# A Winograd convolution pair on one core: two positions of the second convolution also filtered along columns, the map between them kept for two chunks

## The chip, the cores and the metric

The kernel runs on one core of a Trainium2 chip. A core has a matrix engine (TensorE, PE in the profile; PEld is its loading of weights), VectorE (DVE), ScalarE (ACT), GpSimd (POOL), SyncE (SP), which here only issues transfers, and 16 DMA engines. Each engine works through its own list of instructions in the order of the program. All data is fp32; matmuls write to PSUM, everything else stays in SBUF, 128 partitions wide. The metric is the device time of one launch in microseconds, the median of several runs.

## The reference

Four layers on x of shape (4, 256, 56, 56). Layers 0 and 2 are involutions, layer 3 filters in the frequency domain, and each layer normalises its input by group first and adds its result to it. Layer 1 is what the change touches:

```python
h = group_norm(x)
y = conv3x3(h, w1)                      # 256 -> 256 channels, padding 1
y = relu(bn(y, g1, b1, rm1, rv1))
y = conv3x3(y, w2)                      # 256 -> 256
y = bn(y, g2, b2, rm2, rv2)
x = x + relu(h + y)
```

The running statistics of bn are constants, so bn is a scale and a shift for each channel.

## The kernel before

**Where.** `conv_layer` holds layer 1 (L1183 to L1806), from 507 to 1201 us of the span; layer 2 follows. Each image is cut into three row chunks for each convolution, twelve for the four images: `C1_ROWS` 20, 18 and 18 rows, `C2_ROWS` 16, 20 and 20. The order of chunks is conv1(0), then conv1(i) and conv2(i-1) for i from 1 to 11, then conv2(11). So an image's period holds three first and three second chunks.

**Winograd along the rows' width.** A row of 56 is 14 tiles of 4 outputs. `transform` (L1382 to L1425, VectorE) makes six planes of each input row; the 3x3 filters are transformed to six positions in the same way (`row_weights`, `summed_weights`). The product of position k is a sum over 2 blocks of 128 input channels and 3 filter rows, made for 2 blocks of output channels (co); a chunk of n rows has n x 14 columns for each co. The order of positions is `KS` = 1, 2, 3, 4, 0, 5. The output transform puts the six products together to four outputs of each tile. For rows that two chunks share, the transformed planes are copied from the chunk before (`known` rows, L1386 on ScalarE).

**Filtering along columns too.** In the first convolution a position can be "filtered": two output rows come of four products in place of six. It needs sums of input rows: inner ones (row 1 plus row 2, row 2 minus row 1; VectorE, L1464 and L1465) and outer ones (row 0 minus row 2 and row 1 minus row 3; a ScalarE product by -1, L1457, and an accumulating DMA that POOL issues, L1458; for chunk 1 VectorE at L1455). It also needs sums of the filters' rows (`column_weights` on VectorE, L1316 to L1318, and `filter_weights` on ScalarE, L1309). conv1(0) filters none, conv1(1) five positions, all later chunks six. The 16 matmuls of a filtered position are at L1520. Their products come together by a ScalarE copy of the first inner one from PSUM (L1529) and three VectorE operations (L1533, L1534, L1536).

**The second convolution** filters none: 12 matmuls (L1482) for each position, over both co in one PSUM tile for positions 1 to 4, then positions 0 and 5 for co 0, then both for co 1. VectorE combines at L1643 to L1666. Then `joined(co)` sends each half on: ScalarE scales and shifts the four outputs (L1603), POOL adds x by an accumulating DMA (L1604); in the next chunks ScalarE applies the relu (L1606), POOL adds x once more (L1607) and SP stores (L1608). For the last two chunks x is loaded to SBUF beforehand, and `residual` (L1587, ScalarE) makes group norm plus shift in one buffer, from which VectorE goes on (L1611, L1616). The sums for layer 2's norm are `bn_stats` on VectorE (L1633).

**Buffers.** `ph1` holds the normalised input of one chunk (22 rows), written by ScalarE's `phases` (L1379). `ph2` holds the whole image's map between the convolutions (58 rows), written by the first convolution's `outputs` (L1500). Inner sums share four slots, outer sums four. PSUM gives the convolutions four tiles of two banks; a filtered position takes two of these, an unfiltered pair one.

**What sets the order.** There is no scheduler: each chunk has twelve lists of work, `after[0]` to `after[11]`, run after each half position, and work of neighbouring chunks is put into them by `place` and `append` (the loop over `order`). `in_order` then holds each engine to that order of the program. `late_r` carries the relu, addition and store of an output half to the following chunks' lists. SP also issues the loads of input rows (`load_rows`, L1164).

Of the kernel before, what the change touches and what calls it, by code (L numbers as in the profile page):

```python
# [16 lines left out]
P = 128  # L17
B, C, H, W = 4, 256, 56, 56
NB = C // P
# [36 lines left out]
C1_ROWS = [(0, 20), (20, 38), (38, 56)]  # L56
# [16 lines left out]
def net_kernel(  # L73
# [1109 lines left out]
    def conv_layer(xin, xout, st, ahead):  # L1183
        with ExitStack() as es:
# [51 lines left out]
            v2_sb = wpool.tile([P, 2 * NY], F32, name="v2_sb")  # L1236

            def new_v2(half):

                n_v2[half] += 1  # L1240
                at = (n_v2[half] - 1) % 4
                if half:
                    return [room["v2"][:, at * NY : (at + 1) * NY]]
                if at == 3:
                    return [room[r][:, 5 * NY : 5 * NY + NY // 2] for r in ("v2", "xr")]
                t = room["v2"][:, 4 * NY : 5 * NY] if at == 2 else v2_sb[:, at * NY : (at + 1) * NY]
                return [t[:, : NY // 2], t[:, NY // 2 :]]
# [63 lines left out]
            def column_weights(ci, k0, k1):  # L1311

                w0, w1, w2 = (u1_sb[:, ci, y, k0:k1, :] for y in range(3))
                x = between_weights(ci, k0, k1)
                s = y_tile(5 if k0 == 5 else 3)[:, : (k1 - k0) * C].rearrange("p (k n) -> p k n", n=C)
                tt(s, w0, w2, ALU.add)  # L1316
                tt(x, s, w1, ALU.subtract)
                tt(w1, s, w1, ALU.add)  # L1318


            PL, VP = (0, 2, 1, 3), (0, 1, 2, 3, 5, 4)
            ph1 = wpool.tile([P, 4, CV_ROWS + 2, NB, WT + 1], F32, name="ph1")
            ph2 = wpool.tile([P, 4, H + 2, NB, WT + 1], F32, name="ph2")
# [3 lines left out]
            for j in range(4):  # L1327
                for y in (0, H + 1):
                    nc.gpsimd.memset(ph2[:, j, y], 0.0)
# [33 lines left out]
            def phases(i):  # L1363

                y0, y1, lo, hi = rows1(i)
                n, r0, known = y1 - y0 + 2, lo - (y0 - 1), 2 if i % 3 else 0
# [5 lines left out]
                for ci in range(NB):  # L1372
                    at = ci * (CV_ROWS + 2) * W
                    xr = room["rows"][:, at + known * W : at + (hi - lo) * W].rearrange("p (r t j) -> p j r t", t=WT, j=4)
                    for j in range(4):
                        q, t0 = (j + 1) % 4, (j + 1) // 4
                        dst = ph1[:, PL[q], r0 + known : r0 + hi - lo, ci, t0 : t0 + WT]
                        s, t = rstd[:, ci : ci + 1], shift[:, ci : ci + 1]
                        nc.scalar.activation(dst, xr[:, j], AF.Identity, bias=t, scale=s)  # L1379
                        yield  # L1380

            def transform(v, ph, y0, n, known):  # L1382

                if known is not None:
                    old, m = known
                    nc.scalar.copy(  # L1386
                        v[:, :, : 2 * NB].rearrange("p k r t -> p k (r t)"),
                        old[:, :, m * NB : (m + 2) * NB].rearrange("p k r t -> p k (r t)"),
                    )
                    v, y0, n = v[:, :, 2 * NB :], y0 + 2, n - 2  # L1390
# [36 lines left out]
            v_sb = [wpool.tile([P, WPOS, (CV_ROWS + 2) * NB, WT], F32, name=f"v{k}") for k in range(2)]  # L1427

            def input1(i):
# [3 lines left out]
                known = (v_of[1, i - 1], p1 - p0) if i % 3 else None  # L1433
                yield from transform(v, ph1, 0, y1 - y0 + 2, known)

            def input2(i):
                y0, y1 = C2_ROWS[i % 3]
                v = v_of[2, i] = v_sb[i == n_chunks - 1]
                p0, p1 = C2_ROWS[i % 3 - 1]
                known = (v_of[2, i - 1], p1 - p0) if i % 3 else None  # L1440
                yield from transform(v, ph2, y0, y1 - y0 + 2, known)

            def columns(i, k, half):

                y0, y1, _, _ = rows1(i)
                n = y1 - y0
                m = n // 2
                v = v_of[1, i][:, VP[k]]
                if half:
                    (t,) = new_v2(1)  # L1450
                    v = v.rearrange("p r t -> p (r t)")
                    at = slice(0, n * NB * WT)
                    below = slice(2 * NB * WT, (n + 2) * NB * WT)
                    if i == 1:
                        tt(t[:, at], v[:, at], v[:, below], ALU.subtract)  # L1455
                    else:
                        nc.scalar.mul(t[:, at], v[:, below], -1.0)  # L1457
                        nc.gpsimd.dma_start(t[:, at], v[:, at], accum_op=ALU.add)  # L1458
                    t = t.rearrange("p (r e n) -> p e r n", e=2, n=NB * WT)
                    v2_of[i, k, 1] = [t[:, e] for e in range(2)]  # L1460
                else:
                    v = v.rearrange("p (r e c) t -> p e r (c t)", e=2, c=NB)
                    t = v2_of[i, k, 0] = [x.rearrange("p (r n) -> p r n", n=NB * WT) for x in new_v2(0)]
                    tt(t[0][:, :m], v[:, 1, :m], v[:, 0, 1 : m + 1], ALU.add)  # L1464
                    tt(t[1][:, :m], v[:, 0, 1 : m + 1], v[:, 1, :m], ALU.subtract)  # L1465


            FIRST = [(k, half) for k in KS[:4] for half in range(2)]
# [16 lines left out]

            def conv1(i, after, tail):
# [3 lines left out]
                m = n // 2 * WT  # L1490
                a, t, b, s, q = (y_tile(k)[:, : NB * n * WT] for k in (0, 1, 2, 5, 4))
                first = s if i else q
                home = {1: s, 2: q, 3: t, 4: s, 0: y_tile(3)[:, : NB * n * WT], 5: s}

                def outputs(*js):
                    for j in js:
                        o = (a, t, b, q)[j].rearrange("p (c r t) -> p c r t", c=NB, t=WT)
                        p, t0 = PL[(j + 1) % 4], (j + 1) // 4
                        for co in range(NB):
                            nc.scalar.activation(  # L1500
                                ph2[:, p, y0 + 1 : y1 + 1, co, t0 : t0 + WT],
# [7 lines left out]
                for n_s, k in enumerate(KS):  # L1509
                    if k in filtered(i):  # L1510
                        va = v2_of[i, k, 0]
                        vb = v2_of[i, k, 1]
                        ux = [between_weights(ci, k, k + 1)[:, 0] for ci in range(NB)]
                        u0, u1, u2 = ([u1_sb[:, ci, y, k] for ci in range(NB)] for y in range(3))
                        inner, outer = two_banks(), two_banks()
                        work4 = ((inner, 0, va, 0, u1), (inner, 1, va, 1, ux), (outer, 0, vb, 0, u0), (outer, 1, vb, 1, u2))
                        for ps, bank, v2, e, u in work4:
                            for co in range(NB):
                                for ci in range(NB):
                                    nc.tensor.matmul(  # L1520
                                        ps[:, bank, co * m : (co + 1) * m],
                                        u[ci][:, co * P : (co + 1) * P],
                                        v2[e][:, : n // 2, ci * WT : (ci + 1) * WT],
                                        start=(ci == 0),
                                        stop=(ci == NB - 1),
                                    )
                        o = home[k].rearrange("p (r e t) -> p e r t", e=2, t=WT)
                        m1, m2 = (inner[:, e, : NB * m].rearrange("p (r t) -> p r t", t=WT) for e in range(2))
                        nc.scalar.copy(o[:, 0], m1)  # L1529
                        for late in filtered(i)[n_s + 4 : n_s + 5]:  # L1530
                            columns(i, late, 0)
                            columns(i, late, 1)
                        tt(o[:, 1], o[:, 0], m2, ALU.subtract)  # L1533
                        tt(o[:, 0], o[:, 0], m2, ALU.add)  # L1534
                        run_all(after[2 * n_s])
                        tt(o, o, outer[:, :, : NB * m].rearrange("p e (r t) -> p e r t", t=WT), ALU.add)  # L1536
# [30 lines left out]
            def conv2(i, after, sums, tail):  # L1567
# [7 lines left out]
                p, t, r, q = (y_tile(k)[:, : NB * m] for k in range(4))  # L1575
                both = lambda x: x.rearrange("p (c r) -> p c r", c=NB)

                res = ux_sb.rearrange("p c k n -> p (c k n)")[:, : n * W]
                summed = i < n_chunks - 2

                def residual(co):
# [4 lines left out]
                    x = xr_of[i, co][:, : n * W]  # L1586
# [8 lines left out]
                def joined(co):  # L1595

                    y = room["h"][:, : 4 * NY].rearrange("p (j n) -> p j n", j=4)[:, :, co * m : (co + 1) * m]
                    if summed:
# [4 lines left out]
                        nc.scalar.activation(x.rearrange("p (q j) -> p j q", j=4), y, AF.Identity, bias=t, scale=s)  # L1603
                        nc.gpsimd.dma_start(x, xin[bb][co][:, at], accum_op=ALU.add)  # L1604
                        k, by = 5 + 2 * co, rstd[:, co : co + 1]
                        late_r[k].append(lambda: nc.scalar.activation(x, x, AF.Relu, scale=by))  # L1606
                        late_r[k + 1].append(lambda: nc.gpsimd.dma_start(x, xin[bb][co][:, at], accum_op=ALU.add))  # L1607
                        late_r[k + 4].append(lambda: nc.sync.dma_start(xout[bb][co][:, at], x))  # L1608
                        return
                    rj = res.rearrange("p (j q) -> p j q", j=4)  # L1610
# [24 lines left out]
                for n_s, k in enumerate(KS[:4]):  # L1635
                    pair = two_banks()
                    for co in range(NB):
                        unfiltered(pair[:, co, :m], u2_sb, v, k, co, n)
                        if co == 0:
                            run_all(after[2 * n_s])  # L1640
                    got = pair[:, :, :m]
                    if k == 1:
                        nc.scalar.copy(both(q), got)  # L1643
                    elif k == 2:
                        tt(both(p), both(q), got, ALU.add)
                        tt(both(q), got, both(q), ALU.subtract)
# [238 lines left out]
```

## Time and profile before

| | |
|---|---|
| median of 3 runs | 1740.52 us (1738.83 to 1744.15) |
| the profiled execution, its own time | 1735.74 us |
| its span in the profile | 1733.9 us |
| PE busy over the span | 1664.7 us, 96% |
| DVE busy | 1317.1 us, 76% |
| ACT busy | 933.5 us, 54% |
| POOL busy | 476.4 us, 27% |
| L1482, the unfiltered matmuls | 422.8 us |
| L1520, the filtered matmuls | 159.7 us |
| mean granted clock of TensorE | 0.984 |

The page describes one execution. Busy times are summed over the engine's instructions; L1482 is line 1482 of the kernel before. Each matmul of the program appears in the trace as two records, so 12 matmuls are 24 records. The chain that ended last is followed back from the last instruction, each time to what released it; its shares say which lines set the length. A wait is idle time of an engine just before an instruction, put down to what ended it. A window is a stretch of the span, counted from its start, with each engine's busy time in it.

### The profile page before, as it was taken

How to read it: one execution, taken by the hardware profiler on the slowest of the kernel's cores; microseconds unless marked ns; L12 is line 12 of the kernel's file. 1: busy time of each engine (PE TensorE's matmuls, PEld its weight loads, DVE VectorE, ACT ScalarE, POOL GpSimd, SP SyncE). 2: the span in 40 equal slices, each digit the busy share in tenths (PEclk: the TensorE clock that was granted, in tenths of full speed). 3: DMA queues.
4: the chain of work that ended last, by engine and by line, in shares of the span. 5: the costliest groups of instructions: out<-in, count | busy, mean ns of one | idle time of the engine just before them, and what ended most of it. 6: DMA issues, size and time to landing. Idle time of an engine off the chain costs nothing.

```text
span 1733.9 us, 56359 instructions
## 1 busy us (share of the span) xinstructions
PE 1664.7 (96%) x24296; PEld 1479.3 (85%) x24296; DVE 1317.1 (76%) x2467; ACT 933.5 (54%) x2024; POOL 476.4 (27%) x669
## 2 busy tenths in 40 slices
PE   6999999999999999999999999998999899999998
PEld 4998998888977999898899889986988788788886
DVE  2777787777769887798878888856787678778775
ACT  2655556456646455443455245325667567577564
POOL 2223322323334111211122111100000563563571
PEclk9999999999989999999999999999999999999996
DMA  2455444543659546454565354553444666664652
GB/s 89 129 167 162 137 151 160 166 129 103 220 184 260 95 106 142 76 125 96 119 143 97 82 118 92 100 167 104 147 142 151 206 208 196 210 209 161 203 161 103
DMA packets 89030, 252.15 MB, mean 145 GB/s; under 512 B 14453, under 2 KB 35966, under 8 KB 85070
## 3 DMA queue, kind: packets, MB, share of 16 engines
q1 hardware_dynamic: 57438, 163.33, 29.1%
q0 software_dynamic: 30304, 83.95, 22.6%
q8 instruction: 192, 3.15, 0.8%
q10 hardware_dynamic: 1040, 1.26, 0.3%
q14 instruction: 56, 0.46, 0.1%
HBM read 95.07 MB, written 49.15 MB: 83 GB/s over the span
## 4 chain that ended last, share of the span: by engine, by line
PE 70%; DVE 15%; DMA 4%; ACT 4%; issue 3%; SPq 2%; POOL 2%; ACTq 0%; POOLq 0%; DVEq 0%
PE mm L1482 22%; PE ps L593 14%; PE ps L635 14%; PE mm L1520 11%; DVE kt L611 5%; PE ps L407 3%; DVE un L655 3%; DMA xw<-xw 2%; DMA u_sb<-in_wc_dram 2%; PE ps L469 2%; DVE st L1105 1%; ACT hp L488 1%; SPq L425 1%; ACT kt L604 1%; PE ps L718 1%
## 5 line engine op out<-in xcount | busy, mean ns | idle before, releaser
L1482 PE MATMUL mm<-v,u_sb 128*128 128x280 f32 (+2 forms) x1896 | 422.8, 384 | 0.7 <-DVE xs L1534 0.7
L1482 PEld LDWEIGHTS mm<-v,u_sb 128*128 128x128 f32 x1896 | 357.8, 189 | 62.2 <-issue 1.7
L635 PE MATMUL ps<-kt,xw 126*32 126x48 f32 (+1 forms) x12544 | 378.9, 235 | 20.9 <-issue 8.2
L635 PEld LDWEIGHTS ps<-kt,xw 126*32 126x32 f32 (+1 forms) x12544 | 340.6, 121 | 65.8 <-issue 41.5
L593 PE MATMUL ps<-hp,z_sb 64*126 64x133 f32 x6144 | 385.2, 279 | 9.2 <-DVE kt L611 5.0
L593 PEld LDWEIGHTS ps<-hp,z_sb 64*126 64x126 f32 x6144 | 365.1, 186 | 25.7 <-DVE kt L611 7.1
L611 DVE TENSOR_TENSOR kt<-ps,zb_sb 126x798 f32<-126x798 f32 x352 | 333.0, 980 | 59.4 <-PE ps L593 59.0
L604 ACT ACTIVATE kt<-ps,zb_sb 126x133 f32<-126x133 f32 x960 | 281.0, 442 | 108.4 <-PE ps L593 108.4
L655 DVE SCALAR_TENSOR_TENSOR un<-ps,s,un 128x240 f32<-128x240 f32 x224 | 102.4, 457 | 83.4 <-ACT un L650 79.3
L1520 PE MATMUL mm<-xs,u_sb 128*128 128x126 f32 (+1 forms) x1296 | 159.7, 277 | 4.4 <-DVE xs L1534 2.6
L655 DVE SCALAR_TENSOR_TENSOR un<-ps,par_sb,un 128x240 f32<-128x240 f32 x224 | 97.5, 456 | 82.0 <-ACT un L648 78.1
L1520 PEld LDWEIGHTS mm<-xs,u_sb 128*128 128x128 f32 x1296 | 153.3, 191 | 5.4 <-issue 2.9
L660 POOL TENSOR_TENSOR xs<-un,xs 128x240 f32<-128x240 f32 x112 | 72.1, 665 | 216.1 <-DVE un L655 216.1
L419 ACT COPY xw<-ps 126x896 f32<-126x896 f32 x112 | 101.4, 906 | 41.7 <-DMA xw<-xw 22.8
L1458 POOL DMA_DIRECT2D xs<-v x60 | 52.8, 1015 | 249.4 <-ACT xs L1457 248.5
L407 PE MATMUL ps<-ident_sb,strip_sb 128*126 128x128 f32 x784 | 111.6, 282 | 7.7 <-issue 4.3
L150 POOL TENSOR_TENSOR norm_sb<-norm_sb,mhalf 128x1 f32<-128x1 f32 x32 | 19.2, 601 | 360.5 <-DVE norm_sb L149 360.5
L648 ACT ACTIVATE un<-ps,par_sb 128x240 f32<-128x240 f32 x112 | 50.3, 449 | 119.4 <-PE ps L635 109.8
L650 ACT ACTIVATE un<-ps,bn_t,s 128x240 f32<-128x240 f32 x112 | 60.2, 538 | 88.2 <-PE ps L635 80.0
L407 PEld LDWEIGHTS ps<-ident_sb,strip_sb 128*126 128x126 f32 x784 | 84.2, 140 | 19.5 <-issue 5.4
L1603 ACT ACTIVATE xs<-hp,raw,raw 128x1120 f32<-128x1120 f32 (+1 forms) x20 | 45.2, 2260 | 97.7 <-DVE hp L1666 97.7
L1379 ACT ACTIVATE ph<-xs,norm_sb 128x294 f32<-128x294 f32 (+2 forms) x96 | 80.7, 865 | 9.5 <-DMA xs<-x 7.6
(291 smaller groups left out, 2010.0 us busy)
## 6 DMA issues: line engine op xcount, KB each, us to landing
xw<-xw SPq DMA_DIRECT2D x224, 252.0 KB
xw<-xw SPq DMA_DIRECT2D x224, 126.0 KB
xs<-x POOLq DMA_DIRECT2D x26, 560.0 KB, 5.9
x<-xs POOLq DMA_DIRECT2D x8, 1568.0 KB, 8.2
xs<-x SPq DMA_DIRECT2D x8, 1568.0 KB
xs<-v POOLq DMA_DIRECT2D x42, 252.0 KB, 4.2
xs<-in_x_dram SPq DMA_DIRECT2D x6, 1568.0 KB
x<-xs SPq DMA_DIRECT2D x6, 1568.0 KB
```

The source lines that it names most:

```text
L407: nc.tensor.transpose(ps[:Q, k * P : (k + 1) * P], flat[:, k * Q : (k + 1) * Q], ident_sb)
L419: nc.scalar.copy(xw[:, :NSB, :], ps[:Q, : NSB * P].rearrange("q (n c) -> q n c", n=NSB))
L593: nc.tensor.matmul(ps[:Q, i, k * NT : (k + 1) * NT], z_sb[i * R : (i + 1) * R, cb * GB // 2 + gp, z0 : z0 + Q], hp[i * R : (i + 1) * R, py ...
L604: nc.scalar.activation(kt[:, g0 + i, pb, :, k], ps[:Q, i, k * NT : (k + 1) * NT], AF.Identity, bias=zb_sb[:, cb * GB + g0 + i, p0 + k : p0 ...
L611: nc.vector.tensor_tensor(kt[:, g0 : g0 + 2, pb], ps[:Q, :, : PB * NT].rearrange("q i (k t) -> q i t k", k=PB), zb_sb[:, cb * GB + g0 : cb ...
L635: nc.tensor.matmul(v[m * j : m * j + m, i, :, k * TP : (k + 1) * TP], xw[:, window(ty), m * j : m * j + m], kt[:, ng * j : ng * j + ng, :, ...
L650: nc.scalar.activation(part, o[0], AF.Identity, bias=bn["t4"][:, cb : cb + 1], scale=bn["s4"][ng][:, 0, cb : cb + 1])
L655: nc.vector.scalar_tensor_tensor(part, o[e], s, part, ALU.mult, ALU.add)
L660: nc.gpsimd.tensor_tensor(dst, u, dst, ALU.add)
L1379: nc.scalar.activation(dst, xr[:, j], AF.Identity, bias=t, scale=s)
L1482: nc.tensor.matmul(ps, *position(u, v, ci, dy, k, co, n), start=(j == 0), stop=(j == NB * 3 - 1))
L1520: nc.tensor.matmul(ps[:, bank, co * m : (co + 1) * m], u[ci][:, co * P : (co + 1) * P], v2[e][:, : n // 2, ci * WT : (ci + 1) * WT], start ...
```

## The change

Two positions of the second convolution, 4 and 0 (`FILTERED2`), are filtered along columns like those of the first, in all twelve chunks. The product is one function for both convolutions, `filtered_product`. The second filters' row sums are made in conv2(0). Further:

- The inner sums are made for pairs of positions, (1, 2), (3, 4) and (0, 5) of the first convolution and (4, 0) of the second: two VectorE operations for a pair. The pair (1, 2) is kept in two planes of `ph1`. Outer sums have five slots; those of the last chunk lie in the first convolution's weights.
- `C1_ROWS` becomes 18, 20, 18. `ph2` keeps two chunks of 20 rows in turn in place of the image; POOL clears its edge rows for each image, and the second transform copies three known rows, not two. `ph1` has 20 rows.
- Position 0 of the second convolution is made for both co before position 5.
- The first step of `joined` for co 1 moves to the first list of the next chunk, its store one list further; `phases` to lists 4 to 11; `load_rows` to list 11; the transform's steps by a list or so.
- The residual of the last two chunks has a buffer for each co, in the first convolution's weights.

The norm sums stay on VectorE as they were.

```diff
-C1_ROWS = [(0, 20), (20, 38), (38, 56)]
+C1_ROWS = [(0, 18), (18, 38), (38, 56)]
+PH_ROWS = 20
...
+            FILTERED2 = (4, 0)
+            def column_weights2(ci, k):
+                s = y_tile(5)[:, :C]
+                column_sums_of(*(u2_sb[:, ci, y, k, :] for y in range(3)), ux2_sb[FILTERED2.index(k)][:, ci], s)
+            def filter_weights2(ci, k):
+                for w, by in ((u2_sb[:, ci, 1, k], 0.5), (ux2_sb[FILTERED2.index(k)][:, ci], 0.5), (u2_sb[:, ci, 2, k], -1.0)):
+                    nc.scalar.mul(w, w, by)
...
-            ph2 = wpool.tile([P, 4, H + 2, NB, WT + 1], F32, name="ph2")
+            ph2 = wpool.tile([P, 4, 2 * PH_ROWS, NB, WT + 1], F32, name="ph2")
+            def edge_rows(i):
+                for edge, row in ((0, 0), (2, 18)):
+                    if i % 3 == edge:
+                        nc.gpsimd.memset(ph2[:, :, i % 2 * PH_ROWS + row], 0.0)
...
+            def inner_columns(conv, i, *ks):
...
+                tt(t[:, :, 0, :m], v[:, :, 1, :m], v[:, :, 0, 1 : m + 1], ALU.add)
+                tt(t[:, :, 1, :m], v[:, :, 0, 1 : m + 1], v[:, :, 1, :m], ALU.subtract)
+            def outer_columns(conv, i, k):
...
+                if (conv, i) == (1, 1):
+                    tt(t[:, at], v[:, at], v[:, below], ALU.subtract)
+                else:
+                    nc.scalar.mul(t[:, at], v[:, below], -1.0)
+                    nc.gpsimd.dma_start(t[:, at], v[:, at], accum_op=ALU.add)
...
+            def filtered_product(conv, i, k, home, weights, between, items):
...
+                inner, outer = two_banks(), two_banks()
...
+                nc.scalar.copy(o[:, 0], m1)
+                tt(o[:, 1], o[:, 0], m2, ALU.subtract)
+                tt(o[:, 0], o[:, 0], m2, ALU.add)
+                run_all(items)
+                tt(o, o, outer[:, :, : NB * m].rearrange("p e (r t) -> p e r t", t=WT), ALU.add)
...
-                for n_s, k in enumerate(KS[:4]):
...
+                for n_s, k in enumerate(KS[:5]):
+                    if n_s == 4:
+                        residual(0)
+                    if k in filtered2(i):
+                        ux = [ux2_sb[FILTERED2.index(k)][:, ci] for ci in range(NB)]
+                        filtered_product(2, i, k, s, u2_sb, ux, after[2 * n_s])
+                        full, got = (lambda x: x), s
...
+                        tt(full(r), full(t), got, ALU.add)
+                        tt(full(t), full(t), got, ALU.subtract)
...
+                    else:
+                        stt(full(p), full(p), -0.75, got, ALU.mult, ALU.add)
+                        stt(p, r, 0.25, p, ALU.mult, ALU.add)
...
+                        if co == 0:
+                            leaves()
+                        else:
+                            late_r[0].append(leaves)
...
-                            place(after, phases(i + 1), range(1, 10))
+                            place(after, phases(i + 1), range(4, 12))
...
-                                after[9].append(lambda i=i: load_rows(i + 2, xin))
+                                after[11].append(lambda i=i: load_rows(i + 2, xin))
...
+                        after[2].append(lambda i=i: inner_columns(2, i, *filtered2(i)))
+                        for n, k in enumerate(filtered2(i)):
+                            after[2 + n].append(lambda i=i, k=k: outer_columns(2, i, k))
```

## The prediction

> **What bounds the kernel now.** I read the page first (engines, then the chain that ended last), then the chain in order of time between 507 and 1201 us, the only stretch the change touches, then busy time by stage, and last who waits for whom there.
>
> ```profile
> PE 1664.7 (96%) x24296; PEld 1479.3 (85%) x24296; DVE 1317.1 (76%) x2467; ACT 933.5 (54%) x2024; POOL 476.4 (27%) x669
> PE mm L1482 22%; PE ps L593 14%; PE ps L635 14%; PE mm L1520 11%; DVE kt L611 5%; PE ps L407 3%; DVE un L655 3%; DMA xw<-xw 2%; DMA u_sb<-in_wc_dram 2%; PE ps L469 2%; DVE st L1105 1%; ACT hp L488 1%; SPq L425 1%; ACT kt L604 1%; PE ps L718 1%
> ...
> 663.45 22.88 PE mm L1520 x192
> ...
> 1012.99 33.96 PE mm L1482 x144
> 1046.95 21.44 PE mm L1520 x192
> 1068.39 27.25 PE mm L1482 x144
> ```
>
> A third of the chain is the convolutions' matmuls. One unfiltered chunk is 144 records (72 matmuls, each recorded twice): 33.96/144 = 236 ns at 280 columns, 27.25/144 = 189 ns at 224. A filtered chunk is 192: 22.88/192 = 119.2 ns at 140 columns, 21.44/192 = 111.7 ns at 126. By stage (columns: window, its length, then busy us of PE, PEld, DVE, ACT, POOL, clock, DMA share, GB/s), an image's period and its stages:
>
> ```profile
> 883.60:1047.00 163.40, 162.50 (x1019) 148.57 (x1018) 137.15 (x253) 72.71 (x106) 27.73 (x32) 1.00 0.52 110
> 1013.00:1047.00 34.00, 34.00 (x146) 27.26 (x146) 27.70 (x52) 8.20 (x12) 4.40 (x5) 1.00 0.33 84
> 1047.00:1068.40 21.40, 21.40 (x193) 21.40 (x192) 17.68 (x36) 15.96 (x24) 4.36 (x5) 1.00 0.82 154
> 1068.40:1095.60 27.20, 27.20 (x146) 27.18 (x146) 25.17 (x44) 7.41 (x12) 3.47 (x4) 1.00 0.28 61
> ```
>
> TensorE is idle 0.9 us in 163.4; VectorE has 26 us free, and this is where it spends them (720 to 1047 us, two images; us, times, longest):
>
> ```profile
> DVE hp L1665 <- PE mm L1482: 13.8, 11, 1.9
> DVE xs L1533 <- ACT xs L1529: 10.5, 12, 1.5
> DVE hp L1660 <- PE mm L1482: 7.6, 4, 1.9
> PE mm L1520 <- DVE xs L1534: 1.1, 2, 0.5
> ```
>
> VectorE waits for TensorE, hardly the reverse. All its waits there sum to some 46 us, 23 an image.
>
> [...] in the 126-column stage PEld is busy all 21.40 us, at 111.7 ns. So I price 112 columns at 111.7 too; columns alone (0.843 ns each at 280) would give 94. [...] Independent 560-element operations start 0.65 us apart here (978.73, 979.38), dependent ones 0.77. [...] while L1665 waits its 1.9 us, VectorE starts nothing else.
>
> **The change, part by part.**
>
> *A, fewer matmul columns in the second convolution.* A filtered position is 32 records in place of 24. At 20 rows: 24 x 236 = 5.66 us becomes 32 x 119.2 = 3.81, saving 1.85. At 16 rows: 24 x 189 = 4.55 becomes 32 x 111.7 = 3.57, saving 0.98 (1.5 if columns alone set it). Two positions a chunk, eight chunks of 20 rows and four of 16: 8 x 3.70 + 4 x 1.95 = **37.4 us**, or 9.4 an image. The order of instructions shows the 16 matmuls in place.
>
> *B, VectorE's work for it.* A filtered position in the first convolution at 20 rows takes 1.68 us (L1533 at 992.23, L1534, L1536, next at 993.91). Two: 3.36. The paired sums are two 560-element operations, 1.30. Position 0 in one piece instead of by halves: -0.26. So +4.4 at 20 rows, and by the same rates +3.7 at 16. Pairing the first convolution's sums makes six operations of twelve: 12 x 0.33 becomes 6 x 0.59, -0.4 a chunk. An image: 2 x 4.4 + 3.7 - 3 x 0.4 = +11.3; VectorE goes from 137.2 to 148.5 us, against 154.0 for TensorE. Nothing of it costs time while VectorE's waits cover it: new work falls just into the 1.9 us waits at the end of each unfiltered chunk. By stage it doesn't fit (31.9 of work in 30.3 us of 20 rows, 28.4 in 25.3 of 16), but the first convolution gives 4 us back after each, and four double banks let TensorE run two filtered positions ahead. Walking one pair of chunks by these spacings, VectorE ends the second convolution 2 us behind at 20 rows and 4 at 16, and TensorE's next bank is free 0 to 3 us before it is wanted. I take 1.1 us of waits an image: **-4**. Bounds: 0, and see the rivals.
>
> *C, outer sums of those positions.* Two ScalarE products (0.62 us each) and two accumulating DMAs from POOL (0.87 to issue) a chunk. The input is complete 7.5 us into the chunk; product, 0.3 us, and landing put the first sum at about 13 us. L1458 gives the landing:
>
> ```profile
> DMA to landing us min/median/max: 3.3/4.4/7.0
> ```
>
> TensorE wants it after three positions and half of the fourth: 18.9 us at 20 rows, 15.4 at 16. Margins 6 and 2.4 us: nothing. Behind these products on ScalarE stand two for the next first convolution, which wait for VectorE's L1412/L1414, then the copy of position 3, wanted later. ScalarE has 79 of 154 us busy, POOL 33.
>
> *D, moved steps.* The second output half's leaving activation (2.4 us) and its DMA go behind the next chunk's first copy: ScalarE no longer holds L1529 for it. On POOL this DMA now precedes the sums of positions 0 and 5, wanted some 5 us after landing. Its store moves to the next chunk on SP; the row load goes from slot 9 to 11, a chunk before use. Phases move to slots 4 to 11, because their buffer now holds inner sums; eight activations of 0.75 us still precede their first reader by 8 us. Ring of two map chunks: the POOL memsets are of 120 elements, the third kept row adds 0.1 us to a copy. I count D at nothing; its gain could be the 0.9 us idle an image.
>
> *E, the beginning.* First chunk 18 rows, second 20. TensorE saves 144 x (236 - 212) = 3.4 us, then pays 1.8; but VectorE works on weights without a gap from 541 to 564 and TensorE waits 4 us there, so the 3.4 become waiting. Then twelve 256-element operations of 0.44 us (5.3) for the new weights fall into the first 16-row chunk, which already has two sums for the first convolution. There my walk has TensorE wait for banks four times, 4.3 us in all. **-5.5**, between -2 and -8.
>
> *F, the end.* Two result buffers remove the 0.5 us that L1611 waits for L1587. But co 0 and co 1 now follow 2.8 us apart rather than 5.7, and VectorE needs 4.6 for the first: +1.1. The last block load now waits for position 0 of the chunk before, and the residual's load stands behind it on SP: about 1.4 more. **-2.5**.
>
> The norm sums stay L1633, no change. Sum: 37.4 - 4 - 5.5 - 2.5 = **25.4 us**. The profiled execution took 1735.7 us (span 1733.9) and should show about 1708; from the median 1740.5 this is **1715**.
>
> **Rivals.** With VectorE's small gaps (3 us an image) it needs 151.5 plus whatever waiting W stays, against 154.0; so W above 2.5 makes it the bound. The rest is worth 11 periods of three.
>
> *VectorE becomes the bound, W = 7.* 158.5 an image: gain 4.9 x 11/3 = 18, less E and F: 10; **1730**. For it: 96% load, and every filtered position begins with a wait on a ScalarE copy. Against: those waits arise because VectorE is early.
>
> *Slower: VectorE's waits stay as they are.* The six new positions an image each add copy-then-subtract steps; with W = 15 the image takes 166.5, +3.1 x 11/3 + 8 = 19 more: **1760**. It decides at W = 10, where E and F eat the rest. Against: it would need TensorE to wait while VectorE does too, a chain through ScalarE, which is half idle.
>
> *Outer sums late.* If they land 9 us after issue instead of 4.4, TensorE waits at position 4 of the 16-row chunks, and with 2.5 us in each of twelve chunks nothing is left: about **1740**. The longest landing seen is 7.0, but DMA is at 0.8 in the first convolution and the second gets two more transfers.
>
> *Better than I think.* No waits in B, D's idle gone, 112 columns at 96 ns: **1702**.
>
> **The numbers.** My forecast 0.58 (its own range 1706 to 1726), the bound at 1730 0.18, better 0.08, late sums 0.06, slower 0.10. About 0.3% (5 us) is what a measurement can tell. Faster 0.84, within 0.06, slower 0.10. Eight in ten: **1703 to 1732**.
>
> **What would show it.** Right: runs of 96 unfiltered and 64 filtered records in 24.6 + 5.7 us; a period near 155; VectorE busy 148 with hardly a wait on L1482; the first 16-row chunk stretched. Wrong: TensorE waiting on VectorE's or a DMA's release in every second-convolution chunk; a period above 160; filtered 16-row records far from 111.7 ns.

## The result, and the profile after

The changed kernel takes 1730.55 us (median of 8 runs, 1727.57 to 1735.62) against 1740.78 us before (8 runs, 1737.98 to 1744.15): a ratio of 0.9942, 95% interval 0.9927 to 0.9958. It is faster by 10.2 us where 25 were forecast; the time lies at the upper end of the range. The profiled execution took 1727.57 us against 1735.74.

First the chain of the kernel before, by engine; then the page of the changed kernel, its engines and the chain that ended last, by engine and by line (L1525 is the unfiltered matmul, L1540 the filtered one, L1550, L1551 and L1553 VectorE's combining of a filtered position, L1441 to L1455 the transform):

```profile
PE 70%; DVE 15%; DMA 4%; ACT 4%; issue 3%; SPq 2%; POOL 2%; ACTq 0%; POOLq 0%; DVEq 0%
```

```profile
PE 1637.8 (95%) x24488; PEld 1468.4 (85%) x24488; DVE 1359.9 (79%) x2487; ACT 955.2 (55%) x2084; POOL 496.5 (29%) x693
PE 45%; DVE 31%; issue 12%; ACT 5%; DMA 4%; POOL 1%; SPq 1%; ACTq 0%; DVEq 0%; POOLq 0%
PE ps L594 14%; PE ps L636 14%; DVE kt L612 6%; PE mm L1540 4%; PE mm L1525 4%; DVE un L656 3%; PE ps L408 3%; DMA xw<-xw 3%; PE ps L470 1%; DVE v L1451 1%; DVE v L1441 1%; DVE v L1449 1%; DVE xs L1553 1%; DVE st L1688 1%; DVE st L1106 1%
```

TensorE works 27 us less, as the columns say, but the span is only 8.1 us shorter. In the chain the convolutions' matmuls fell from 33% to 8%, and VectorE rose from 15% to 31%, much of it small operations: TensorE has begun to wait for VectorE. Where it waits is seen by stage. Each window is one image's period, then three second-convolution chunks (the first of 20 rows after an image's third first-convolution chunk, a regular one of 20 rows, one of 16), then the last chunk; columns as before (length, busy us of PE, PEld, DVE, ACT, POOL, granted clock, DMA share, GB/s):

```profile
876.67:1036.65 159.98, 156.95 (x1066) 145.87 (x1065) 145.73 (x253) 77.18 (x118) 33.36 (x40) 0.98 0.58 123
949.89:983.44 33.55, 33.55 (x163) 27.98 (x163) 30.41 (x50) 7.04 (x14) 5.25 (x6) 0.91 0.40 81
1006.51:1036.78 30.27, 30.27 (x163) 25.77 (x162) 29.79 (x49) 8.67 (x16) 5.22 (x6) 1.00 0.51 126
1059.66:1085.35 25.69, 25.53 (x161) 25.02 (x159) 25.24 (x41) 7.76 (x16) 5.00 (x6) 1.00 0.35 73
1142.13:1183.31 41.18, 33.45 (x162) 28.43 (x161) 18.01 (x32) 13.84 (x11) 5.72 (x8) 0.88 0.44 109
```

The regular chunk takes 30.3 us, exactly as forecast (24.6 + 5.7), the 16-row one 25.7. The last chunk takes 41.2 with TensorE idle for 7.7 of them, and at a mean clock of 0.88; the first one listed takes 33.6 at a clock of 0.91. So I set the layer against the forecast stage by stage. The layer runs from the start of layer 0's last transpositions (505.5 us before, 509.4 after) to layer 2's first matmul (1201.2 and 1199.6). The forecast column lays the parts A to F out by stretch; chunks that lost or gained rows carry that too:

| stretch | before | forecast change | measured change |
|---|---|---|---|
| layer start to conv1(2) | 102.4 | +3.5 | +1.2 |
| conv1(2) to conv1(4) | 112.2 | -8.0 | -8.5 |
| two images, conv1(4) to conv1(10) | 326.7 | -16.5 | -6.7 |
| conv1(10) to conv2(11) | 105.3 | -3.2 | +0.3 |
| conv2(11) to layer 2 | 49.2 | -1.2 | +8.3 |
| the layer | 695.7 | -25.4 | -5.5 |

Some 10 us were lost in the two images, 3.5 in the piece of an image after them, and 9.5 at the end. Outside the layer the two executions differ by another 2.6 us.

**In each image** TensorE makes no convolution matmul for 2.8 us, before the chunk at 949.9. The same place in the image before, by the timeline (start, length, engine, line; in brackets the idle time and what ended it), and then what the kernel before did there:

```profile
786.54 1.95 PE L1540 MATMUL mm<-xs,u_sb 128*128 128x126 f32 x16
788.25 0.67 DVE L1553 TENSOR_TENSOR hp<-hp,mm 128x504 f32<-128x504 f32 x1
788.97 0.38 PE L219 MATMUL mm<-mv,gavg_sb 128*128 128x1 f32 x2 [0.36 <-DVE hp L1553]
790.71 0.42 DVE L1551 TENSOR_TENSOR xs<-xs,mm 128x252 f32<-128x252 f32 x1
791.28 0.47 PE L1525 MATMUL mm<-v,u_sb 128*128 128x280 f32 x1 [1.92 <-DVE xs L1551]
```

```profile
790.25 0.51 PE L218 MATMUL mm<-mv,gavg_sb 128*128 128x1 f32 x4
790.98 34.20 PE L1482 MATMUL mm<-v,u_sb 128*128 128x280 f32 x144 [0.23 <-DVE xs L1534]
```

The matmuls end at 788.5. Then come two tiny ones, L219 (four records), the norm of the image before: in the rotation of four PSUM tiles they take the two that position 0 has just given back. The next chunk's first product gets the tile of position 5, which VectorE frees only at 791.1, 2.6 us after the matmuls ended. In the kernel before the same two matmuls stand at the same place and TensorE waits 0.23 us after them. So the tiles alone do not cost it; they cost where VectorE is late.

**In the last chunk** TensorE waits for a DMA. POOL's timeline in that stretch (L1681 adds x to chunk 10's result, L1682 stores it, L1508 makes the outer sums):

```profile
1150.32 0.88 POOL L1681 DMA_DIRECT2D xs<-x  x1 [28.20 <-ACT xs L1680]
1156.45 0.57 POOL L1682 DMA_DIRECT2D x<-xs  x1 [5.26 <-DMA xs<-x]
1157.05 0.86 POOL L1681 DMA_DIRECT2D xs<-x  x1
1164.15 0.55 POOL L1682 DMA_DIRECT2D x<-xs  x1 [6.24 <-DMA xs<-x]
1164.69 1.77 POOL L1508 DMA_DIRECT2D u_sb<-v  x2
```

ScalarE's products (L1507) were ready at 1153.6. Their DMAs are issued at 1164.7, behind two stores that each wait for an addition to land, and TensorE goes on at 1169.0:

```profile
PE mm L1540 <- DMA u_sb<-v: 7.7, 1, 7.7
```

### The profile page after: what moved, and what is told of

Its sections match the earlier page's. It is cut to its first block, busy times and chain, and to the rows that moved or that the text cites. A ratio compares the mean times of both kernels' runs of the same rounds, so it can differ in the third digit from the quotient of the medians.

```text
span 1725.8 us, 56946 instructions
## 1 busy us (share of the span) xinstructions
PE 1637.8 (95%) x24488; PEld 1468.4 (85%) x24488; DVE 1359.9 (79%) x2487; ACT 955.2 (55%) x2084; POOL 496.5 (29%) x693
## 4 chain that ended last, share of the span: by engine, by line
PE 45%; DVE 31%; issue 12%; ACT 5%; DMA 4%; POOL 1%; SPq 1%; ACTq 0%; DVEq 0%; POOLq 0%
PE ps L594 14%; PE ps L636 14%; DVE kt L612 6%; PE mm L1540 4%; PE mm L1525 4%; DVE un L656 3%; PE ps L408 3%; DMA xw<-xw 3%; PE ps L470 1%; DVE v L1451 1%; DVE v L1441 1%; DVE v L1449 1%; DVE xs L1553 1%; DVE st L1688 1%; DVE st L1106 1%
## 5 line engine op out<-in xcount | busy, mean ns | idle before, releaser
L594 PEld LDWEIGHTS ps<-hp,z_sb 64*126 64x126 f32 x6144 | 366.0, 186 | 25.4 <-DVE kt L612 7.1
L1525 PE MATMUL mm<-v,u_sb 128*128 128x280 f32 (+2 forms) x1320 | 301.9, 389 | 6.8 <-DVE xs L1551 6.8
L1525 PEld LDWEIGHTS mm<-v,u_sb 128*128 128x128 f32 x1320 | 252.2, 193 | 49.8 <-ACT ph L1411 4.0
L1540 PE MATMUL mm<-xs,u_sb 128*128 128x126 f32 (+2 forms) x1392 | 174.3, 278 | 0.6 <-DMA xs<-v 0.6
L1540 PEld LDWEIGHTS mm<-xs,u_sb 128*128 128x128 f32 x1392 | 166.7, 191 | 0.9 <-DVE xs L1553 0.7
L1508 POOL DMA_DIRECT2D xs<-v x82 | 75.2, 1016 | 312.9 <-ACT xs L1507 249.0
L420 ACT COPY xw<-ps 126x896 f32<-126x896 f32 x112 | 101.4, 906 | 41.2 <-PE ps L408 21.2
L1411 ACT ACTIVATE ph<-xs,norm_sb 128x266 f32<-128x266 f32 (+2 forms) x96 | 80.8, 868 | 9.6 <-DMA xs<-x 7.8
L1507 ACT ACTIVATE xs<-v 128x504 f32<-128x504 f32 (+2 forms) x82 | 51.1, 639 | 52.1 <-DVE v L1443 23.7
```

Of the source, the lines that this page charges most:

```text
L420: nc.scalar.copy(xw[:, :NSB, :], ps[:Q, : NSB * P].rearrange("q (n c) -> q n c", n=NSB))
L594: nc.tensor.matmul(ps[:Q, i, k * NT : (k + 1) * NT], z_sb[i * R : (i + 1) * R, cb * GB // 2 + gp, z0 : z0 + Q], hp[i * R : (i + 1) * R, py ...
L1525: nc.tensor.matmul(ps, *position(u, v, ci, dy, k, co, n), start=(j == 0), stop=(j == NB * 3 - 1))
L1540: nc.tensor.matmul(ps[:, bank, co * m : (co + 1) * m], u[ci][:, co * P : (co + 1) * P], v2[:, : n // 2, ci * WT : (ci + 1) * WT], start=(c ...
```

## The experiments

All start from the changed kernel unless told otherwise. Ratios are to the kernel before, run beside them. The expectations name three theories: V, VectorE's work bounds the image; P, the norm's matmuls take two of the four PSUM tiles where VectorE is late; Q, the last chunk's outer sums stand in POOL's queue. "Layer" and "image" are from the one trace of each: the layer as above, and the two periods conv1(4) to conv1(7) to conv1(10).

| run | median us | ratio, 95% interval | layer | image |
|---|---|---|---|---|
| changed kernel | 1730.55 | 0.9942 (0.9927 to 0.9958) | 690.2 | 160.0, 160.0 |
| the same again | 1727.74 | 0.9917 (0.9886 to 0.9948) | 686.0 | 158.6, 157.4 |
| last outer sums by VectorE | 1718.34 | 0.9874 (0.9848 to 0.9900) | 679.4 | 160.1, 158.5 |
| light norm sums | 1711.84 | 0.9845 (0.9822 to 0.9868) | 673.7 | 154.1, 154.1 |
| light norm sums in the kernel before | 1738.81 | 0.9986 (0.9969 to 1.0004) | 695.0 | 163.4, 163.4 |
| 16-row chunks unfiltered | 1728.64 | 0.9930 (0.9909 to 0.9952) | 679.1 | 156.4, 156.4 |
| norm steps at lists 3, 5, 7 | 1722.33 | 0.9907 (0.9884 to 0.9930) | 684.1 | 158.7, 157.5 |
| both leaving steps late | 1728.19 | 0.9932 (0.9914 to 0.9949) | 691.5 | 159.8, 161.1 |
| three waits away | 1712.02 | 0.9838 (0.9817 to 0.9859) | 672.7 | 158.1, 156.7 |
| + inner sums by POOL | 1733.39 | 0.9954 (0.9939 to 0.9970) | 692.7 | 163.7, 160.9 |
| + sums by ScalarE | 1708.05 | 0.9801 (0.9768 to 0.9834) | 667.4 | 154.1, 154.1 |
| the last, norm steps at 5, 11 | 1716.06 | 0.9849 (0.9823 to 0.9875) | 678.9 | 158.3, 159.4 |
| three waits away, norm at 1, 3, 4 | 1712.34 | 0.9832 (0.9809 to 0.9855) | 671.3 | 155.4, 156.2 |
| the last + sums by ScalarE | 1701.19 | 0.9767 (0.9746 to 0.9789) | 664.9 | 152.5, 152.5 |

### The end: who makes the last outer sums

```diff
-                if (conv, i) == (1, 1):
+                if (conv, i) in ((1, 1), (2, n_chunks - 1)):
```

> The changed kernel with the two outer sums of the last chunk made by VectorE (two subtractions of 560) in place of ScalarE and an accumulating DMA. Theory Q (POOL's queue): the 7.7 us that TensorE waits in the last chunk come from those DMAs standing on POOL behind two stores that wait for an addition to land; the wait goes, and the 10 us at half clock after it: last chunk 32 to 33 us for 41.2, launch 1721 to 1724. Rival (the residual's loads, late on SP, set the end): TensorE is done sooner, but layer 2 starts no more than 2 us sooner, launch 1728 to 1731.

The last chunk, by window:

```profile
1140.98:1171.49 30.51, 30.51 (x162) 25.68 (x161) 17.82 (x33) 11.30 (x9) 4.47 (x6) 1.00 0.48 128
```

No idle, full clock, 30.5 us for 41.2, and 1718 us in all, below the 1721 to 1724 of theory Q. From conv2(11) to layer 2 it is 48.2 us, what the forecast had (49.2 - 1.2), and the layer 10.8 us shorter than in the first trace. Theory Q holds in kind. In this trace ScalarE still waits up to 9.4 us for the residual's loads; they did not set the end.

### VectorE's load

In `stats`, in the changed kernel and in the kernel before:

```diff
-                    nc.vector.bn_stats(sums[co][:, at, :], xr_of[i, co][:, r0 * W : r1 * W])
+                    nc.vector.bn_stats(sums[co][:, at, :], xr_of[i, co][:, r0 * W : r0 * W + W])
```

> The changed kernel with each of the norm sums over one row of 56 elements in place of up to eight rows (448), so that VectorE has about 6.7 us less to do an image; the statistics of layer 2 are then those of part of the rows. Theory V (VectorE's work bounds the image): an image takes 153.5 to 155 us for 160.0, with no idle of TensorE before a second-convolution chunk, launch 1712 to 1716. Theory P (PSUM tiles taken by the norm's matmuls): most of the 2.8 us idle stays, 158 us an image, launch 1724 to 1728.

> The kernel before, with each of its norm sums over one row of 56 elements in place of up to eight rows, so that VectorE has some 6.7 us less to do an image; layer 2's statistics are then those of part of the rows. Theory V (VectorE's work bounds the changed kernel only; the kernel before is bounded by TensorE): an image stays at 163 us and the launch within 0.3% of the kernel before. Rival (norm sums cost their time in either kernel): 157 us an image, launch 1715 to 1725.

An image of the changed kernel with light sums:

```profile
866.27:1020.33 154.06, 152.90 (x1065) 143.69 (x1064) 140.41 (x253) 77.18 (x118) 33.33 (x40) 1.00 0.61 128
```

VectorE is 5.3 us less busy an image in both. This is worth 3.3 to 5.9 us an image and some 17 us in all (0.9942 less 0.9845) after the change, and nothing that can be told from noise before it. So the change did move the limit to VectorE's side. The norm's matmuls still stand at their old places here, and the pause there is 1.4 us in place of 2.8: relief alone takes half of it away. The third dose:

```diff
             def filtered2(i):
-                return FILTERED2
+                return FILTERED2 if i % 3 else ()
```

From the second 16-row chunk on, these chunks multiply by filter rows that were already combined in place, so what they compute for positions 4 and 0 is not the convolution; the work is that of unfiltered positions.

> The changed kernel with no position filtered in the four second-convolution chunks of 16 rows; those of 20 rows filter both. TensorE gets 1.95 us more a chunk, VectorE some 3.7 us less just where it is late. Theory V: the 2.8 us idle that follows and the half clock after it go: 157 us an image for 160.0, launch 1717 to 1722. Theory P (PSUM tiles alone): the idle stays at 2 us or more, an image takes 161 us or more, launch 1730 to 1735.

An image takes 156.4 us, against 157 by theory V, and the long pause before the next chunk is gone. The launch missed theory V's 1717 to 1722: it stayed at 1728.6. In its trace layers 0, 2 and 3 take 1049.0 us together, against 1031 to 1044 in the others. Why they are longer in this kernel stays open. The layer itself became 11.1 us shorter than in the first trace, so its length is the sharper measure here.

### The norm's two PSUM tiles

```diff
-                for g in slow:
-                    after[5].append(step(g))
-                    after[11].append(step(g))
+                for g in slow if conv == 2 else ():
+                    for k in (3, 5, 7):
+                        after[k].append(step(g))
```

> The changed kernel with the steps of the norm of the image before moved out of the first convolution: they run only in second-convolution chunks, at lists 3, 5 and 7, while positions 2, 3 and 4 are made. Theory P (PSUM tiles): the 2.8 us that TensorE idles before every third second-convolution chunk is there because the norm's two small matmuls take two of the four PSUM tiles just when VectorE is late; they gone, the idle goes, and with it the 3.4 to 6.8 us at half clock[...]. An image then takes 155 to 156 us for 160.0, the launch 1714 to 1718. Theory V (VectorE's work bounds the image): the same work is still to be done, the wait turns up at another place, an image keeps 158 to 160 us and the launch 1727 to 1731.

The wait went from its old place and came up at a new one, which the timeline shows (TensorE alone):

```profile
960.44 0.50 PE L219 MATMUL mm<-mv,gavg_sb 128*128 128x1 f32 x4
960.80 1.20 PE L1540 MATMUL mm<-v_sb,u_sb 128*128 128x140 f32 x8
961.84 1.12 PE L1540 MATMUL mm<-v_sb,ux 128*128 128x140 f32 x8
962.79 2.07 PE L1540 MATMUL mm<-xs,u_sb 128*128 128x140 f32 x16
967.36 0.83 PE L1540 MATMUL mm<-v_sb,u_sb 128*128 128x140 f32 x5 [2.49 <-DVE xs L1551]
```

The norm's matmuls now take two tiles just ahead of a filtered position that takes the other two; the next filtered position waits 2.5 us. That the wait turns up elsewhere is what theory V said; the launch, 1722, lies between the two ranges. The theories are not told apart by that. Next, with the end mended too (last outer sums by VectorE) and layer 2's first load in list 8 of chunk 10:

> The changed kernel with three of its waits taken away together: norm steps in second-convolution chunks only, the last chunk's outer sums by VectorE, and the load of layer 2's first blocks put behind the residual's loads on SP (list 8 of chunk 10 in place of 2). If the gains add, as different stages should: 1728 less 6, less 10, and 0 to 3 for the residual, which VectorE awaits 4.8 us at the end of chunk 10: 1709 to 1714. Rival (the tail's end is set by the last residual load alone): 1717 to 1720.

The launch, 1712, is in the range: the gains add. It is also close to the 1715 forecast for the change as such, with VectorE's work left as it is. Then the norm sums of the first three images by ScalarE, once with the norm steps at 3, 5, 7, once at their old places 5 and 11:

```diff
+                    if i // 3 < B - 1:
+                        if k < 2:
+                            half = n // 2 * W
+                            for j, f in enumerate((AF.Identity, AF.Square)):
+                                nc.scalar.activation(
+                                    room["v2"][:, 5 * NY : 5 * NY + half // 2].bitcast(mybir.dt.bfloat16),
+                                    xr_of[i, co][:, k * half : (k + 1) * half],
+                                    f,
+                                    accum_out=sums[co][:, i % 3 + 3 * k, j : j + 1],
+                                )
+                        return
```

> The kernel with the three waits taken away (norm steps moved, the last chunk's outer sums by VectorE, layer 2's first load later), and the norm sums of the first three images made by ScalarE in place of VectorE: for each half of an output half chunk one activation that sums and one that sums squares, four a co, in lists 4 and 5 of the next second-convolution chunk. VectorE has 9 to 10 us less to do an image, ScalarE some 15 more. Theory V (VectorE's work bounds the image): 153.5 to 154.5 us an image for 157 to 158, launch 1698 to 1704. Rival (ScalarE's copies and products now come late): TensorE or VectorE waits on ScalarE, 157 us an image or more, launch 1710 or more.

> The same with the norm steps back in their old lists (5 and 11 of every chunk). Theory V: with VectorE early the two PSUM tiles that they take cost TensorE 1 us an image or less, as in the run with light norm sums; launch within 4 us of the run with the steps moved. Theory P (PSUM tiles): TensorE waits 2 us or more before every third second-convolution chunk, launch 8 us or more above it.

The first brought 154.1 us an image, as theory V said; the launch, 1708, stayed 4 us above its range. The second is a miss for V: VectorE is busy 139.8 us in a period, as little as with light sums (140.4), but TensorE waits 1.9 us at the old place again, an image takes 158 to 159, and the launch is 8.0 us longer, as theory P had it. It does not show the tiles' part alone, though: ScalarE's sums need six small VectorE operations a co where one was before, 2.2 us for both in place of 0.6, and with the steps at their old places they fall into just that late chunk. Hence the last pair, norm steps at lists 1, 3 and 4, ahead of unfiltered positions, without and with ScalarE's sums:

> The kernel with three waits taken away, but the norm's steps placed otherwise: in lists 1, 3 and 4 of second-convolution chunks, so that the four PSUM tiles after its matmuls are not both of a filtered position that VectorE has just begun. VectorE's work is the same as in the changed kernel. Theory P (PSUM tiles taken where VectorE is late): the 2.5 us idle that the steps at lists 3, 5 and 7 left before position 0 goes too, an image takes 154 to 155.5 us, launch 1699 to 1705. Theory V (VectorE's work as such bounds the image): 156.5 us or more, launch 1709 or more.

> The same placing of the norm's steps, and the norm sums of the first three images made by ScalarE. Theory P: little is left to gain, 153.5 to 154.5 us an image, launch within 3 us of the run with the sums left on VectorE. Theory V: 154 us an image, launch 6 us or more below that run.

An image of each, by window:

```profile
872.42:1028.63 156.21, 153.76 (x1065) 143.74 (x1064) 145.94 (x256) 77.10 (x118) 34.04 (x40) 1.00 0.60 126
```

```profile
870.20:1022.70 152.50, 152.50 (x1066) 143.49 (x1065) 139.70 (x247) 93.14 (x166) 34.73 (x40) 1.00 0.61 129
```

With VectorE's work the same in amount, the other places for the norm's steps bring an image from between 157.4 and 160.0 us down to 155.4 and 156.2. The launch, 1712.3, is no better than with lists 3, 5 and 7, and lies in theory V's range, not in P's. TensorE still waits in each image, 1.7 us in the second, now before position 5 of the 16-row chunk, where no norm matmul stands: there VectorE is simply late. Relieving VectorE brings another 2.9 to 3.7 us an image, down to 152.5, where no wait of TensorE is left, and 11 us of launch, against P's "within 3" and as V's "6 or more" had it. So both causes are there, and they overlap: light sums alone, with the tiles at their old places, had already brought 154.1. The runs do not give each a share of its own, also because moving the steps moves 0.6 us of VectorE's norm work out of the late chunk along with the tiles. This last kernel is the fastest of all: 0.9767 of the time before.

### ScalarE's order

```diff
-                        if co == 0:
-                            leaves()
-                        else:
-                            late_r[0].append(leaves)
+                        late_r[0].append(leaves)
```

> The changed kernel with the first step of joined for co 0 also moved behind the first copy of the next chunk, as the change does for co 1. Theory S (ScalarE's order): VectorE's 1.6 us wait on the copy of the next chunk's first position, which stands behind this activation of 2 us, goes; as VectorE is behind there, an image gains 1 to 2 us, launch 1723 to 1727. Rival: VectorE spends the time later anyway, on the second activation and the copy of the known rows behind it, launch 1729 to 1732.

No gain. The wait only moved from the first to the second of these lines (VectorE in the changed kernel, then in this one):

```profile
772.79 0.42 DVE L1550 TENSOR_TENSOR xs<-xs,mm 128x252 f32<-128x252 f32 x1 [1.63 <-ACT xs L1549]
```

```profile
773.98 0.74 DVE L1441 SCALAR_TENSOR_TENSOR v<-ph 128x560 f32<-128x560 f32 x1 [1.63 <-ACT v L1417]
```

The copy of the known rows, L1417, now stands behind both leaving steps. The rival was right in kind; its 1729 to 1732 was missed by 0.8 us.

### Inner sums by POOL

```diff
-                tt(t[:, :, 0, :m], v[:, :, 1, :m], v[:, :, 0, 1 : m + 1], ALU.add)
-                tt(t[:, :, 1, :m], v[:, :, 0, 1 : m + 1], v[:, :, 1, :m], ALU.subtract)
+                add = nc.gpsimd.tensor_tensor if conv == 2 else tt
+                add(t[:, :, 0, :m], v[:, :, 1, :m], v[:, :, 0, 1 : m + 1], ALU.add)
+                add(t[:, :, 1, :m], v[:, :, 0, 1 : m + 1], v[:, :, 1, :m], ALU.subtract)
...
```

Both outer sums also move to list 2, ahead of these additions.

> The kernel with those three waits taken away, and the inner sums of the second convolution's two positions added by POOL, two operations of 560 a chunk, after its outer sums' DMAs; VectorE has 4.2 us less to do an image. Theory V: an image takes 154 to 155.5 us, launch 1699 to 1705. Rival (POOL's additions, some 1.5 us each, hold up its DMAs for the next first convolution or come late for position 4): TensorE waits on POOL or a DMA, launch 1710 or more.

It cost 21 us. VectorE's busy time an image rose from 145.7 to 150.3 us, though it had six operations less, and it is VectorE that TensorE waits for, up to 2.8 us at a time, not POOL or a DMA as the rival had it. The timeline says why:

```profile
701.57 2.03 POOL L1492 TENSOR_TENSOR v_sb<-v 128x560 f32<-128x560 f32 x1
701.96 3.57 DVE L1443 TENSOR_TENSOR v<-v 128x560 f32<-128x560 f32 x1
702.90 2.02 POOL L1493 TENSOR_TENSOR v_sb<-v 128x560 f32<-128x560 f32 x1
705.45 0.73 DVE L1445 TENSOR_TENSOR v<-v 128x560 f32<-128x560 f32 x1
```

In the changed kernel L1443 takes 0.7 us. Here it takes 3.57: until just after POOL is through. It ended at 705.53, only after both of POOL's, which cover 3.4 us (701.57 to 704.92). Of the 24 operations of L1443 the longest took 3.85 us in this kernel and 0.74 in the changed one. Why an operation takes longer beside POOL's additions is not shown.

### The same kernel again

> The changed kernel once more, for a second trace. If its execution is the same but for the time of DMAs in layers 0, 2 and 3 and the place of the half-clock stretches, the convolution layer takes 688 to 692 us again (690.2 in the first trace, 695.7 in the kernel before) and an image 159 to 161; launch 1727 to 1732. If the layer itself varies from execution to execution, its length differs by 4 us or more.

The layer is 4.2 us shorter than in the first trace, with the same 2.8 us pauses. The chunk after the pause in the second image, this time:

```profile
948.24:978.75 30.51, 30.51 (x163) 26.02 (x163) 29.85 (x49) 7.14 (x14) 5.22 (x6) 1.00 0.44 89
```

30.5 us at full clock, where the first trace had 33.6 at 0.91. Counted from the span's start, the clock's records have half speed from 949.2 to 956.1 us in the first trace, directly at the end of the pause: its matmuls start 467 ns apart up to 956, then 236 ns. The second trace, at 1.00 in this chunk, has none there. So the layer does vary from execution to execution, in this image by whether a pause is followed by half speed. In the first image, 160.0 us against 158.6, both have a mean clock of 0.99 (3.4 us at half speed in the first trace, from 792.2); there the difference is two waits of TensorE, 0.55 and 0.73 us, of which the second trace has 0.16. But for the one that ends the launch, the stretches at half speed last 3.4, 6.8 or 10.2 us in the first trace and in that of the kernel before. In the first trace each of the three pauses of 2.8 us, with 1.9 us idle in one piece, goes with half speed, which begins at 792.2, 949.2 and 1109.7 us, within 0.9 us of the pause's end; these are its only such stretches that begin between 600 and 1140 us. In the second trace the pause at 948 us has none after it, and in the first trace neither has one of 1.9 us at 611. The kernel before, whose longest wait of TensorE in that stretch is 0.5 us, has no half speed there. In the second image of other kernels the mean clock is 1.00 with light sums (longest wait 1.1 us) and in the last kernel (no wait), 0.99 with the norm's steps at 3, 5 and 7 (2.5 us), 0.98 with ScalarE's sums and the steps at 5 and 11 (1.9 us), but also 1.00 with the inner sums by POOL (2.8 us). No run changed the pause alone, so this is what goes together, not a shown cause.

## Why the prediction was right and wrong

- **A, the columns: right.** A 20-row chunk fell from 34.1 to 30.4 us, 3.7 as forecast; a 16-row chunk without waits takes 25.5 for 27.4, 1.9 for the 1.95.
- **B, VectorE's work: the size of it right, what it costs wrong.** VectorE is busy 145.7 to 147.1 us an image (148.5 forecast). "I take 1.1 us of waits an image" is the step that failed: it was 3.4 to 6.0 us in the two traces, measured from the forecast's 154.0 for TensorE. Even that floor was too high: in the last kernel, where TensorE doesn't wait, an image takes 152.5, so 4.9 to 7.5 us were lost. The forecast let TensorE run two filtered positions ahead on four tiles and did not count that the norm's two matmuls take two of the four, once an image, in the chunk where VectorE is late. The runs with other places for the norm's steps and the runs with less work for VectorE show that each has a part, and the last run that nothing is left when both are mended; how the loss divides between them stays open. Nor did it count the half clock that followed some of the pauses.
- **C, outer sums: right for eleven chunks, wrong for the last.** "Margins 6 and 2.4 us: nothing" was taken from a regular chunk. In the last, POOL first has chunk 10's additions and stores, and each store holds it until an addition has landed, 5.3 and 6.2 us. This costs 9.2 us (57.4 from conv2(11) to layer 2, 48.2 with those sums by VectorE), nearly all of what F is short. The chunk itself is 10.7 us longer: 7.7 of waiting, and 2.9 more of matmuls, at half clock after the wait (half speed from 1164.3 to 1174.5 us; matmuls go on at 1169.0).
- **D, moved steps: not tested by themselves.** The run that moved co 0's leaving step tried one more such move, not those of the change; it gained nothing.
- **E, the beginning: a little better than thought.** E's cost of 5.5 us less A's gain of 1.95 in the first 16-row chunk makes +3.5; measured was +1.2.
- **F, the end: right in itself.** With the outer sums out of the way, it is 48.2 us for the 48.0 forecast.
- **The rivals.** "VectorE becomes the bound" with 158.5 us an image and 1730 in all came nearest: 157.4 to 160.0, and 1730.55. Its mechanism is only half of it. VectorE had 13 to 14 us free in a period of 160 us; it is not its sum that bounds, but being late at some places, the more so where tiles are short. And that its total agrees is luck: it did not have the loss at the end, and what makes up for that lies at the beginning and in part outside the layer (2.6 us in the first pair of traces). Outer sums did come late, in one chunk instead of twelve, and not by the slow landing of that rival: TensorE went on 4.3 us after they were issued, but they were issued late.

## What to carry to other kernels

Margins taken from the regular stage don't hold for the last one: list what else stands on each queue there, above all instructions that wait for a DMA to land. When two engines that feed each other come close (here 146 us of VectorE's work an image beside 152.5 of TensorE's), count the buffers between them at every place, with the tiny users too; other places for a norm's steps with their four 1-column matmuls brought an image from between 157.4 and 160.0 us to 155.4 and 156.2. And before work goes from VectorE to POOL, look at whether VectorE's operations then take longer (here 3.57 us in place of 0.7).

## What had not been expected of the hardware

A VectorE operation of 560 elements took 3.57 us in place of 0.7 while POOL made two additions of some 2.0 us each. Pauses of TensorE of 2.8 us, of which 1.9 in one piece, were followed, in some executions, by 3.4 to 6.8 us at half clock that began within 0.9 us of the pause's end, worth 1.7 to 3.0 us. Layers 0, 2 and 3, whose work the changes leave as it is, took 1031 to 1049 us together in single executions, so one execution says little of a change of 10 us.
